# Moving the quarter sums of weights to VectorE inside the scan's slots, and one PSUM bank swapped

## The chip, the cores and the metric

The kernel runs on one core of a Trainium2 chip. The metric is the device time of one execution in microseconds. TensorE (PE in the profile, its weight loads PEld) multiplies matrices, VectorE (DVE) and GpSimd (POOL) do elementwise work, ScalarE (ACT) does activations and scaled copies, and SyncE (SP) issues the DMAs, in one queue, in order.

## The reference

One layer of a network: a layer norm of x (2048 tokens by 1024 channels, float32), then the sum of x, a state-space block and a feed-forward block with routed low-rank adapters, both fed with the normed x.

```python
xn = layernorm(x)
# state-space block: 64 heads of 64, state 128, 8 groups of B and C
proj = xn @ in_proj_w.T                 # gate 4096 | x, B, C 6144 | dt 64
xBC  = silu(causal_conv4(proj[xBC]) + conv_bias)
dt   = softplus(proj[dt] + dt_bias);  dA = exp(-dt * exp(A_log))
state = state * dA_t + (dt_t * x_t) B_t ;  y_t = state C_t    # over tokens t
y = y + x * D
y = groupnorm_rms(y) * norm_weight * silu(gate)
attn = y @ out_proj_w.T
# feed-forward: base product, and the two best of 8 adapters of rank 16
w = softmax over the top 2 of xn @ W_router.T
ffn = xn @ W_base.T + b_base + sum_e w_e * (xn A_e.T) B_e.T * 2
out = x + attn + ffn
```

## The kernel before

**Sections, blocks, slots.** The 2048 tokens lie in two sections of 1024. A section has, for each of the 8 groups, two halves of 512 tokens; section, group and half make a block, 32 in all. A block has four chunks of 128 tokens, c = 0 to 3. One chunk is a slot of the main loop, 128 slots in all. A slot takes some 14 to 18 us.

**Products with seven instead of eight parts.** The large products are made by a scheme of the Strassen kind: a pair of weight tiles is taken as a 2 x 2 matrix of quarters a11, a12, a21, a22, and seven products (PSUM tiles ps_a, ps_x, ps_y) of sums of quarters replace eight. The sums of the weights are s1 = a21 + a22, s2 = s1 - a11, s3 = a11 - a21 and s4 = a12 - s2. A quarter is 128 x 512 float32, 256 KB. In the first section such sums are made on GpSimd as the weights come (L465) and are kept in DRAM.

**What a slot does.** TensorE gets three to five of the seven-part products of the projection (`products`, L81), and among them the scan of the chunk. `scan_a` prepares the next chunk: the scan of the decays es on VectorE (L749, from dab, loaded by DMA and broadcast), ps_cb on TensorE (B times C, and a transpose of B), copies cbm and bt out of it on ScalarE (L760, L762), D times x into ps_y on ScalarE (L767), the masking product of es and cbm on VectorE (L772, kept in the list `masked`), then transposes ps_xt, and xdt and xdd on ScalarE (L784, L792). `scan_b` finishes the chunk: ps_y, then ps_e (C times the state), then ps_st on TensorE; on VectorE ecp times ps_e (L831), the sum with ps_y into xg (L832), and the state (L846), whose decay is a product on GpSimd (L85 with state,tot). In the slots of c = 1 to 3 the convolution of the next block runs: a scaled copy on ScalarE (L698), three steps on VectorE for each of six tiles (L704), a silu on ScalarE (L692). In the slots of c = 3 and 0 the finished block is squared and normed (L872, L875, L876, ps_nv on TensorE, L884 with a table load on ScalarE, L890, L893, L903) and stored.

**Order.** TensorE's instructions keep the order of the program. On VectorE those that are passed to `pin` keep their order among themselves; the scheduler puts the others between them. `behind(a, b)` makes an instruction come after another in the order, with no wait on a semaphore. On GpSimd `gp(1, ...)` keeps the order of the program.

**The quarter sums in question.** Twelve slots, 53 to 64 (the four of each of the last three blocks of the first section), also make sums of weights for later: four pairs of W_base (`base_sums`, tiles wb) and eight pairs of gate weights (`oct_sums`, tiles ws). The generator `quad_sums` has three steps: four loads into one of two "quad" tiles, four sums in place, four stores (L919, L85, L928). The four loads are issued at the end of the slot before, the sums follow `scan_b` in the program's order of the slot, and the stores come at its end, ahead of the next four loads. Four more pairs of gate weights (o = 2) are summed much later, outside the slots. The sums of the output projection's weights, `out_sums`, run from slot 65 on, four on GpSimd and four on VectorE behind the masking product.

**The step sizes' product.** In the last slot of a block, four times in the first section (slots 8, 20, 32 and 44), a piece of the next section's tokens is multiplied with the 200 columns of weights for dt, the router and the adapters: ps_sm, 5.4 us of products, then a copy on ScalarE (L1191). Its PSUM bank has the tag "aux", which ps_cb, ps_nv and the sums of the layer norm use too. The bank with the tag "e" holds ps_e.

## Time and profile before

| | |
|---|---|
| time, median of 3 runs | 3407.71 us (3406.72 to 3408.86) |
| the profiled execution's own time | 3409.37 us |
| its span in the profile | 3407.6 us, at a mean granted clock of 0.996 |
| PE busy | 3351.6 us (98%) |
| DVE busy | 2474.4 us (73%) |
| ACT busy | 1522.1 us (45%) |
| POOL busy | 779.9 us (23%) |
| GB/s, mean | 235 |

How to read it: a share is an average over stages. The slots end near 2100 us of the span; the 48 sums that the change moves run on GpSimd from 999.8 to about 1194 us, and ps_sm stands at 297.0, 484.4, 674.1 and 865.1 us. "A <- B" in a line of waits says that A was idle until B ended. The profile's line numbers are those of the kernel before. L81 and L85 are lines of helpers (every product, every GpSimd sum through `gp`), so tiles tell more there than lines.

### The profile page before, as it was taken

How to read it: one execution, taken by the hardware profiler on the slowest of the kernel's cores; microseconds unless marked ns; L12 is line 12 of the kernel's file. 1: busy time of each engine (PE TensorE's matmuls, PEld its weight loads, DVE VectorE, ACT ScalarE, POOL GpSimd, SP SyncE). 2: the span in 40 equal slices, each digit the busy share in tenths (PEclk: the TensorE clock that was granted, in tenths of full speed). 3: DMA queues.
4: the chain of work that ended last, by engine and by line, in shares of the span. 5: the costliest groups of instructions: out<-in, count | busy, mean ns of one | idle time of the engine just before them, and what ended most of it. 6: DMA issues, size and time to landing. Idle time of an engine off the chain costs nothing.

```text
span 3407.6 us, 41304 instructions
## 1 busy us (share of the span) xinstructions
PE 3351.6 (98%) x13828; PEld 2181.4 (64%) x13828; DVE 2474.4 (73%) x2640; ACT 1522.1 (45%) x4030; POOL 779.9 (23%) x547
## 2 busy tenths in 40 slices
PE   9999999999999999999999999999999999999999
PEld 7455554555554445555555554688888888888888
DVE  7379888889888788898898897555644565556554
ACT  2256766676666566666666664222222200000000
POOL 4122222222214421121212121475444100000000
PEclk9999999999999999999999999999999999999999
DMA  6656666666689988989898899666655787585654
GB/s 247 198 162 220 196 201 194 205 202 200 200 281 312 311 271 272 273 247 290 245 280 254 267 288 303 208 223 232 225 184 185 257 305 242 200 300 179 216 165 144
DMA packets 535571, 799.38 MB, mean 235 GB/s; under 512 B 34880, under 2 KB 264384, under 8 KB 531776
## 3 DMA queue, kind: packets, MB, share of 16 engines
q1 hardware_dynamic: 535360, 796.75, 72.7%
q8 instruction: 111, 1.82, 0.2%
q14 instruction: 100, 0.82, 0.1%
HBM read 546.00 MB, written 250.61 MB: 234 GB/s over the span
## 4 chain that ended last, share of the span: by engine, by line
PE 77%; DVE 12%; ACT 4%; DMA 3%; issue 3%; SPq 0%; POOL 0%; DVEq 0%; ACTq 0%; POOLq 0%
PE ps_x_x L81 11%; PE ps_x_w L81 9%; PE ps_a_x L81 7%; PE ps_y_x L81 7%; PE ps_a_w L81 6%; PE ps_y_w L81 6%; PE ps_x_z L81 5%; DVE xg L704 3%; PE ps_y_z L81 3%; PE ps_a_z L81 3%; PE ps_e L81 3%; PE ps_y L81 3%; PE ps_st L81 2%; PE ps_x_b L81 2%; DVE es L749 2%
## 5 line engine op out<-in xcount | busy, mean ns | idle before, releaser
L85 POOL TENSOR_TENSOR state<-state,tot 128x512 f32<-128x512 f32 x112 | 137.3, 1226 | 951.8 <-PE ps_e L81 898.3
L704 DVE SCALAR_TENSOR_TENSOR xg<-rawx,cw,xg 128x512 f32<-128x512 f32 x384 | 342.2, 899 | 16.8 <-ACT xg L698 5.9
L749 DVE TENSOR_TENSOR_SCAN es<-dab,here 128x1024 f32<-128x1024 f32 x128 | 297.8, 2326 | 14.5 <-DMA dab<-da_d 10.2
L81 PE MATMUL ps_x_w<-t,w 128*128 128x256 f32 x1344 | 303.8, 379 | 0.0
L767 ACT ACTIVATE ps_y<-xg,dsk 128x128 f32<-128x128 f32 x512 | 189.7, 370 | 225.2 <-DVE xg L832 190.0
L81 PEld LDWEIGHTS ps_x_w<-t,w 128*128 128x128 f32 x1344 | 255.4, 190 | 41.5 <-issue 7.4
L792 ACT ACTIVATE xdd<-xdt,es 128x64 f32<-128x64 f32 x1024 | 262.6, 392 | 1.3 <-DVE es L749 1.3
L784 ACT ACTIVATE xdt<-ps_xt,dt 128x64 f32<-128x64 f32 x1024 | 223.8, 337 | 59.1 <-PE ps_xt L105 58.9
L81 PE MATMUL ps_a_w<-q,w 128*128 128x256 f32 x896 | 204.3, 381 | 3.4 <-DMA w<-w 3.4
L704 DVE SCALAR_TENSOR_TENSOR bc<-rawb,cw,bc 128x512 f32<-128x512 f32 x192 | 191.0, 1001 | 18.4 <-ACT bc L698 15.0
L1680 ACT COPY ps_x_w<-ps_a_w 128x512 f32<-128x512 f32 x28 | 16.0, 570 | 420.8 <-PE ps_a_w L81 420.8
L81 PEld LDWEIGHTS ps_a_w<-q,w 128*128 128x128 f32 x896 | 171.3, 191 | 27.4 <-issue 3.8
L81 PEld LDWEIGHTS ps_y<-dab,xdt 128*64 128x64 f32 x2048 | 111.3, 136 | 104.0 <-ACT xdd L792 88.9
L81 PE MATMUL ps_a_x<-op_again,a_x 128*128 128x512 f32 x384 | 176.1, 602 | 0.0
L81 PE MATMUL ps_y_x<-op_again,s_x 128*128 128x512 f32 x384 | 174.4, 597 | 0.0
L81 PE MATMUL ps_x_x<-op_again,s_x 128*128 128x512 f32 x384 | 172.7, 592 | 0.0
L772 DVE TENSOR_TENSOR dab<-es,cbm 128x1024 f32<-128x1024 f32 x128 | 164.8, 1287 | 10.3 <-ACT cbm L760 10.0
L81 PE MATMUL ps_a_x<-op,a_x 128*128 128x512 f32 x368 | 165.5, 592 | 0.0
L81 PE MATMUL ps_y_x<-op,s_x 128*128 128x512 f32 x368 | 165.5, 592 | 0.0
L81 PE MATMUL ps_x_x<-op,s_x 128*128 128x512 f32 x368 | 165.5, 592 | 0.0
L465 POOL TENSOR_TENSOR s_x<-a_x,a_x 128x512 f32<-128x512 f32 x48 | 74.3, 1548 | 363.6 <-PE ps_y_x L81 218.5
L831 DVE TENSOR_TENSOR ecp<-ecp,ps_e 128x512 f32<-128x512 f32 x120 | 81.8, 682 | 103.9 <-PE ps_e L81 97.8
(322 smaller groups left out, 6769.5 us busy)
## 6 DMA issues: line engine op xcount, KB each, us to landing
w<-w SPq DMA_DIRECT2D x196, 512.0 KB, 3.7
dab<-da_d SPq DMA_DIRECT2D x128, 512.0 KB, 6.5
raw<-ev SPq DMA_DIRECT2D x192, 256.0 KB, 4.3
a_x<-in_w_in_dram SPq DMA_DIRECT2D x168, 256.0 KB, 4.9
w<-wo SPq DMA_DIRECT2D x96, 448.0 KB, 4.9
ecp<-run_d SPq DMA_DIRECT2D x256, 128.0 KB, 6.0
y<-xg SPq DMA_DIRECT2D x64, 512.0 KB, 4.5
rawx<-raw SPq DMA_DIRECT2D x24, 1030.0 KB, 7.0
```

The lines of the kernel that those rows point to most:

```text
L81: tc.keep_in_program_order(nc.tensor.matmul(*args, **kw))
L85: ins = nc.gpsimd.tensor_tensor(*args)
L465: nc.gpsimd.tensor_tensor(t[what], t[x], t[y], alu)
L704: ins = nc.vector.scalar_tensor_tensor(dst[:, i, :], raw[:, i, k : k + TB], cw[:, ti, k : k + 1], dst[:, i, :], ALU.mult, ALU.add,)
L749: ins = nc.vector.tensor_tensor_scan(es.rearrange("p h t -> p (h t)"), dab.rearrange("p h t -> p (h t)"), here, 0.0, ALU.mult, ALU.add,)
L767: nc.scalar.activation(psy[:, j, :], xg[:, j, cs], AF.Copy, scale=dsk[:, at : at + 1])
L772: nc.vector.tensor_tensor(ms, es, cbm.unsqueeze(1).to_broadcast([P, HG, Q]), ALU.mult)
L784: ins = nc.scalar.activation(xdt[:, h, :], x_t[:, h, :], AF.Copy, scale=dt_of[s][:, half * NQ + c, at : at + 1],)
L792: ins = nc.scalar.activation(xdd[:, h, :], xdt[:, h, :], AF.Copy, scale=es[:, h, Q - 1 : Q])
L831: pin(nc.vector.tensor_tensor(ecp, ecp, pse, ALU.mult))
L1680: nc.scalar.copy(px, pa)
```

## The change

Three things are edited.

- `quad_sums` takes the function that makes a sum. `base_sums`, and `oct_sums` for o = 0 and 1, pass `add_in_slot`: a sum on VectorE, ordered behind the slot's masking product and pinned. The four pairs of o = 2 stay on GpSimd. `out_sums` uses the new helper for its four VectorE sums; what it makes is the same, but the first of them alone had been ordered behind the masking product, and now all four are.
- The step of the sums in a slot moves from behind `scan_b` to the list `parts[2]`, that is, into the product after the masking product.
- ps_sm moves from the bank "aux" to the bank "e".

In the built program TensorE's order is the same. On VectorE the 48 sums stand, in each slot, behind L772 and what is pinned of the convolution or the norm around it, ahead of L831; in the slot at 1053 us of the old trace the four sums and the copy L829 now stand ahead of the next scan L749, and in the slot at 1110 us the quarter sum L569 of ps_x_x stands ahead of L832, the state and the scan. On GpSimd only the state products are left in the twelve slots. In SyncE's queue one store of the first pair goes ahead of two stores of y.

```diff
+    def add_in_slot(*args):
+
+        ins = nc.vector.tensor_tensor(*args)
+        behind(ins, masked[0])
+        pin(ins)
+
-    def quad_sums(t, quarters, to):
+    def quad_sums(t, quarters, to, add):
...
-        yield from quad_sums(t, halves(w_base[2 * i], w_base[2 * i + 1]), to)
+        yield from quad_sums(t, halves(w_base[2 * i], w_base[2 * i + 1]), to, add_in_slot)
...
-    def oct_sums(pool, o, i):
+    def oct_sums(pool, o, i, add=add):
...
-        yield from quad_sums(t, halves(w_in[at], w_in[at + 2]), to)
+        yield from quad_sums(t, halves(w_in[at], w_in[at + 2]), to, add)
...
-        ins = nc.vector.tensor_tensor(x, t0, t2, ALU.subtract)
-        behind(ins, masked[0])
-        pin(ins)
-        pin(nc.vector.tensor_tensor(t2, t2, t3, ALU.add))
-        pin(nc.vector.tensor_tensor(t0, t2, t0, ALU.subtract))
-        pin(nc.vector.tensor_tensor(t1, t1, t0, ALU.subtract))
+        add_in_slot(x, t0, t2, ALU.subtract)
+        add_in_slot(t2, t2, t3, ALU.add)
+        add_in_slot(t0, t2, t0, ALU.subtract)
+        add_in_slot(t1, t1, t0, ALU.subtract)
...
-                quads += [oct_sums(wq, o, k) for o in range(2) for k in range(4)]
+                quads += [oct_sums(wq, o, k, add_in_slot) for o in range(2) for k in range(4)]
...
             scan_b(*blk, c)
             if c == 0 and prev:
                 norm_mean(*prev)
-            if 0 < q <= len(quads):
-                next(quads[q - 1])
...
                 if b >= 16:
                     parts[2] += [lambda: next(left_sums)]
+            if 0 < q <= len(quads):
+                parts[2] += steps(quads[q - 1], 1)
             products(1, parts[1])
             next(a, None)
             products(1, parts[2])
...
-                ps = ps_one.tile([P, 2, NSM], F32, tag="aux", name=f"ps_sm_{piece[1]}")
+                ps = ps_one.tile([P, 2, NSM], F32, tag="e", name=f"ps_sm_{piece[1]}")
```

## The prediction

> **What bounds the kernel now.** I read the page first, then the stages, the waits of TensorE, and single stretches of the timeline. Two lines of the page, busy time and the chain that ended last:

> ```profile
> PE 3351.6 (98%) x13828; PEld 2181.4 (64%) x13828; DVE 2474.4 (73%) x2640; ACT 1522.1 (45%) x4030; POOL 779.9 (23%) x547
> PE 77%; DVE 12%; ACT 4%; DMA 3%; issue 3%; SPq 0%; POOL 0%; DVEq 0%; ACTq 0%; POOLq 0%
> ```

> TensorE bounds the kernel as a whole, and its order of instructions is the same in both programs. So the change can only win what TensorE loses near the two edits: idle time, and time at half clock. The answer by stages shows both. The columns are the length, the busy time (and count) of PE, PEld, DVE, ACT and POOL, then the granted clock, the DMA share and GB/s. The four short rows are stretches at half clock; the long one holds all 48 sums that the change moves:

> ```profile
> 674.10:677.50 3.40, 3.38 (x10) 3.39 (x11) 2.63 (x3) 3.40 (x15) 0.00 (x0) 0.50 0.96 305
> 1063.20:1066.60 3.40, 3.40 (x5) 1.35 (x5) 3.40 (x2) 1.22 (x5) 0.00 (x0) 0.50 1.05 399
> 1114.40:1121.20 6.80, 5.84 (x7) 2.52 (x8) 5.42 (x6) 0.84 (x4) 0.93 (x1) 0.50 1.02 354
> 1182.70:1186.10 3.40, 3.40 (x5) 1.35 (x4) 2.01 (x2) 3.37 (x12) 0.00 (x0) 0.50 1.06 342
> 985.00:1200.00 215.00, 204.53 (x773) 102.94 (x772) 171.07 (x159) 129.15 (x371) 87.93 (x60) 0.97 0.93 303
> ```

> The waits of TensorE in that long stretch (total us, times, longest):

> ```profile
> PE ps_x_x L81 <- DVE ev L569: 3.7, 1, 3.7
> PE ps_cb L81 <- ACT rms L884: 3.3, 1, 3.3
> PE ps_xt L105 <- DVE state L846: 1.4, 3, 1.1
> PE ps_xt L105 <- ACT xg L692: 1.3, 1, 1.3
> PE ps_y L81 <- ACT xdd L792: 0.7, 1, 0.7
> ```

> They sum to 10.4 us. The half clock costs half of 3.4 + 6.8 + 3.4 us, another 6.8. So TensorE loses 17.2 us among the 48 sums, and VectorE, or ScalarE behind VectorE, ends nearly all of it. Why VectorE is late there shows in the timelines of VectorE and GpSimd (start, length, what, count):

> ```profile
> 1082.42 3.77 DVE L704 SCALAR_TENSOR_TENSOR bc<-rawb,cw,bc 128x512 f32<-128x512 f32 x5
> ...
> 1089.62 4.98 DVE L704 SCALAR_TENSOR_TENSOR xg<-rawx,cw,xg 128x512 f32<-128x512 f32 x3 [3.43 <-DMA raw<-ev]
> ```

> ```profile
> 1089.43 6.31 POOL L85 TENSOR_TENSOR ws<-ws 128x512 f32<-128x512 f32 x4
> ```

> The same convolution step takes 0.75 us while GpSimd rests and 1.66 us while GpSimd sums weights. VectorE's operations that read PSUM (L831, L832, L846) stay at 0.68 us beside GpSimd. Two more rows carry the prices, of the weight sums on GpSimd and of a VectorE sum of this very shape:

> ```profile
> L85 POOL TENSOR_TENSOR wb<-wb x16: 1260/1539/3126, 999.8 to 1057.5; 128x512 f32<-128x512 f32 x16
> ```

> ```profile
> L876 DVE TENSOR_TENSOR sq<-sq x32: 666/683/685, 237.2 to 2119.9; 128x512 f32<-128x512 f32 x32
> ```

> The second edit is about two waits on TensorE's timeline:

> ```profile
> 671.90 0.44 PE L105 MATMUL ps_xt<-ident,xg 128*128 128x128 f32 x2 [0.98 <-ACT xg L692]
> 674.12 2.37 PE L81 MATMUL ps_sm<-wsm,piece 128*128 128x200 f32 x6 [1.77 <-ACT bt L762]
> ...
> 865.10 1.11 PE L81 MATMUL ps_sm<-wsm,piece 128*128 128x200 f32 x5 [1.53 <-ACT bt L762]
> ```

> **Part one: the bank of the step sizes.** ps_sm runs four times, at 297.0, 484.4, 674.1 and 865.1 us. In bank "aux" it waits until ScalarE has copied cbm and bt out of ps_cb. TensorE has no gap before the first two, 1.77 and 1.53 us before the others. In bank "e" its predecessor is ps_e, which VectorE reads at L831. That was done at 859.8 for the last one, and by 668.8 for the third, 5 us early: no wait is left. The price could come at the other end, since the next ps_e now waits for ScalarE's copy of ps_sm (L1191, 0.49 us). That copy began within 0.4 us of the last product's end, and ps_e comes one product of 3.44 us and ps_y of 1.02 us later: covered by over 3 us. Idle 3.30 us; the half clock after the third (its 0.98 us wait stays, and single gaps of 1.1 us elsewhere, at 480.4, drew none) is half of 3.4, 1.7. Sum 5.0 us. [...]

> **Part two: the 48 sums.** Twelve slots, four sums each, leave GpSimd, which keeps only the state's products (L85, 1.04 us alone). VectorE gains 48 x 0.683 = 32.8 us. It loses the slowing: L704 took 16.93, 19.54 and 18.87 us for 18 each in 985-1060, 1060-1130 and 1130-1200, against 27.46 us for 36 in 880-985, so 55.3 - 41.2 = 14.1 us; the gated norm's L893 took 4.83, 3.74 and 4.75 us for four against 2.72 without GpSimd at 1202.7, so 5.2 us; L903 3.20 and 4.50 against 2.35 for two, so 3.0 us. Net +10.5 us: 171.1 to 181.6 us of a stretch that would shrink from 215 to about 198 us, 92%. That is close, but 1200-1320 us has 107.7 of 120 (90%) and loses one gap of 2.0 us. The price of a sum is bounded by 0.68 (GpSimd at rest) and 1.37 us (doubled, as L704 is); I take 0.68, since only one state product a slot is left there.

> No row shows the new sums' own wait. They stand in VectorE's queue behind the masked product (L772), after the conv steps or norm around them, and wait for four loads issued at the end of the slot before; behind a waiting sum stand the conv steps, ecp, xg, the state and the next scan, and behind those ScalarE's ps_y and TensorE's transposes. When the loads had landed shows where GpSimd waited for them, against the end of the VectorE work that now stands ahead: 999.8 against 1006, 1022.5 against 1021.7, 1038.7 against 1038.7, 1053.5 against 1052.0, 1068.6 against 1072, 1102.9 against about 1104, 1132.7 against 1139, 1189.2 against 1188.5. So it waits 0 to 1.5 us, and the 1.5 lies inside a wait of 4.54 us for dab. In the slots of 1086 and 1155 the sums fill waits of 3.43 and 4.07 us that VectorE has before the xg steps.

> What each place of loss becomes:
> - 1062.59, 3.26 us and 1.7 at half clock. The chain was: dab lands late, the scan runs at 1056.58, and only behind it the copy xg L829 at 1059.47, ps_y, a table load, rms at 1061.85, ps_cb. In the new order the copy stands before that scan, behind the four sums: sums from 1053.5 to 1056.2, copy to 1056.9, ps_y, table load and rms (0.37 + 1.28 + 0.69) to 1059.3, just when TensorE gets there (1059.3). Won: 5.0.
> - 1096.6 to 1115.4, 0.17 + 0.72 + 3.73 and 3.4 at half clock. VectorE's xg steps ran 4.98 us for three and 8.89 for seven. Unslowed they are 2.2 and 5.2; the first slot's sums lie in the 3.43 us wait, the second's add 2.7. So ev arrives about 2.8 + 3.7 - 2.7 = 3.8 us earlier by this alone, and the new order sets it ahead of the scan and the squares. Won 7.3, with the 0.72 for ScalarE's xdd left in place.
> - 1165.1 to 1182.2, 0.17 + 1.06 + 1.31 and 1.7 at half clock. Steps of 4.54 for three and 9.45 for eight become 2.2 and 5.9, with one slot's sums uncovered: 2.3 + 3.5 - 2.7 = 3.1 us against 2.5 us of waits. That is thin: I count half, 2.1.

> SyncE's queue moves with it. The stores L928 waited 26.5 us in all for GpSimd's ws sums, with the next loads, dab, ecp and raw behind them. At 1090.7 to 1096.1 they will go some 6 us earlier; where a norm is in the slot, one store goes ahead of the two of y, and the rest follow as before. The bytes are the same. VectorE's four waits for the state product behind the sums (6.9 us up to 1215) go too. [...] The state products mostly run while VectorE does ecp and xg, which read PSUM; the longest took 3.39 us.

> Sum: 5.0 + 5.0 + 7.3 + 2.1 = 19.4; I take off 2.0 for small new waits (the 0.5 to 0.8 us landings above): 17.4 us. The profiled execution took 3409.37 us, 3407.6 of span and 1.8 around it; it becomes 3392.0. It lies 1.7 us over the median of 3407.71, which becomes 3390.3 us.

> **Rivals.**
> 1. VectorE becomes the bound of the conv slots. Scan 2.2, masked product 1.1, nine steps 6.7, two ev 1.2, ecp, xg and state 1.9 are 13.1 us; the sums make 15.8, where TensorE's slot with three products is about 14.1. For it: six such slots. Against it: in the old trace ecp ran 6.2 us behind ps_e at 1094.5 before a transpose waited 0.17 us, so two slots in a row stay inside the slack. If so, the bank and 1062.59 win 10, the rest nothing: 3398.
> 2. The sums change nothing: their waits come back elsewhere, and the bank's 5.0 is all: 3402.7.
> 3. Slower: the loads land late. Median landing of ws is 5.0 us, the longest 10.7; at 94% DMA share more can be late. From about 1 us later than in the old trace, VectorE stands still at the slots of 1022, 1038 and 1189, where no other wait covers it, and TensorE follows past the slack of 6 us. At 10.7 us each is 4.5 us late: 13.5, and the bank's gain: 3416.
> 4. The half clock stays, drawn by the small waits that are left, such as the 0.98 us one at 671.9: 8.5 us less, 3398.8, counted in with rival 1. Or the bank's wait is only passed on to ps_e: 3395, inside the forecast's spread.

> **How the numbers follow.** A measurement here can tell about 0.2%, 6.8 us, from no change. Forecast, gains of 12 to 23 us: 0.56. Rival 1: 0.17. Rival 2: 0.15. Rival 3: 0.12. Faster is 0.56 + 0.17 = 0.73, same 0.15, slower 0.12. The low end is all 22.2 us and the 2.0 us gap at 1229.2 with some of its half clock: 3383. The high end takes in rival 2 with two thirds of its spread: 3407. It leaves out rival 3 and some 0.06 of the others.

> **What would show it.** Right: L704 back near 0.75 us between 985 and 1200; GpSimd's L85 rows wb gone, VectorE's there at 0.68; no TensorE gap over 1 us at the four places, no half clock there; ps_sm without a wait; VectorE near 182 us in the stretch. Wrong: VectorE waiting for wb or ws loads by more than 2 us with TensorE waiting behind it; ps_e waiting for L1191; the gap at 1115 still there behind ev.

## The result, and the profile after

The changed kernel takes 3399.77 us (median of 8 runs, 3392.98 to 3403.31), and the kernel before, run beside it, 3408.28 us (3406.72 to 3413.09). The ratio is 0.997, with a 95% interval of 0.9959 to 0.9981. The kernel is faster, by 8.5 us where 17.4 were forecast. The profiled execution took 3401.96 us, 3400.1 of it span.

The two lines of the page, busy time and the chain that ended last, stand nearly as before; VectorE has 15 us more, GpSimd 77 us less:

```profile
PE 3344.5 (98%) x13828; PEld 2178.1 (64%) x13828; DVE 2489.8 (73%) x2688; ACT 1523.0 (45%) x4030; POOL 703.3 (21%) x499
PE 72%; DVE 14%; DMA 6%; ACT 5%; issue 3%; SPq 0%; POOL 0%; DVEq 0%; ACTq 0%; POOLq 0%
```

TensorE executes the same instructions in the same order in both programs, so each of its instructions can be set against itself in the other trace: its start after minus its start before is the **shift**. The work between 985 and 1200 us of the old trace lies between 990.78 and 1190.34 of the new one. The answer by stages for that stretch (length, busy time and count of PE, PEld, DVE, ACT, POOL, then granted clock, DMA share, GB/s), and below it the waits of TensorE there:

```profile
990.78:1190.34 199.56, 197.94 (x774) 101.24 (x773) 184.58 (x208) 129.74 (x374) 14.70 (x12) 1.00 1.00 332
```

```profile
PE ps_xt L105 <- DVE state L846: 1.1, 1, 1.1
PE ps_y L81 <- ACT xdt L784: 0.4, 1, 0.4
```

215 us have become 199.6, its three half-clock stretches of 3.4 to 6.8 us are gone (the clock is 1.00), and 10.4 us of waits have become 1.5. VectorE is busy 184.6 us of it, 92%. The groups of the convolution step and of the sums (minimum, median and maximum in ns; L918 is the line of `add_in_slot` in the changed kernel):

```profile
L704 DVE SCALAR_TENSOR_TENSOR xg<-rawx,cw,xg x37: 724/752/1414, 984.4 to 1170.2; 128x512 f32<-128x512 f32 x37
L918 DVE TENSOR_TENSOR wb<-wb x16: 679/691/928, 1012.1 to 1059.9; 128x512 f32<-128x512 f32 x16
L918 DVE TENSOR_TENSOR ws<-ws x32: 678/692/1521, 1073.1 to 1182.1; 128x512 f32<-128x512 f32 x32
```

So in this stretch nearly everything went as forecast; of the waits named beforehand one is left, the 1.06 us before a transpose (at 1180.5 us before, at 1173.0 now). The shift tells where the rest of the gain went. It is +2.9 us at 660 us, where nothing has been edited yet: that is the difference of two executions. Behind the third ps_sm it falls to -1.0, and at 709 us it is +3.1 again. Behind the fourth it falls from 3.8 to 2.0, and is 5.8 at 936 us. Through the sums it falls from +5.8 to -10.2 and by 1234 to -12.2, since the half clock behind the wait at 1229 is gone (the wait itself only shrank, from 2.0 to 1.7 us); it is -9.7 at 1290 and -7.8 at the end. **The sums won about as much as forecast; the bank's gain was won twice and lost twice, each time within 70 us.** At the fourth ps_sm twice as much was lost as won, 3.8 us against 1.8. TensorE's timeline at these places:

```profile
674.91 5.58 PE L81 MATMUL ps_sm<-wsm,piece 128*128 128x200 f32 x32
...
692.42 0.49 PE L81 MATMUL ps_cb<-bc 128*128 128x128 f32 x2 [2.12 <-ACT rms L884]
...
902.90 3.70 PE L81 MATMUL ps_x_x<-op,s_x 128*128 128x512 f32 x8 [0.89 <-ACT s_x L520]
...
937.22 0.63 PE L105 MATMUL ps_xt<-ident,xg 128*128 128x128 f32 x4 [2.52 <-DVE state L846]
```

ps_sm waits no more, and 18 us behind it TensorE waits 2.12 us for the norm's rms, then runs 3.4 us at half clock (693.3 to 696.7). VectorE's and ScalarE's timelines show what rms waited for:

```profile
680.98 2.29 DVE L749 TENSOR_TENSOR_SCAN es<-dab,here 128x1024 f32<-128x1024 f32 x1 [1.96 <-ACT xdd L792]
683.19 0.27 DVE L337 TENSOR_TENSOR scr<-sm,dtb 128x128 f32<-128x128 f32 x1
...
688.43 0.15 DVE L427 TENSOR_TENSOR m_b<-m_b,m_a 128x2 f32<-128x2 f32 x1
688.50 0.68 DVE L829 COPY xg<-ps_y 128x512 f32<-128x512 f32 x1
```

```profile
689.22 0.37 ACT L767 ACTIVATE ps_y<-xg,dsk 128x128 f32<-128x128 f32 x1 [2.12 <-DVE xg L829]
...
690.39 1.28 ACT L884 ACT_TABLE_LOAD   x1
691.68 0.69 ACT L884 ACTIVATE rms<-ps_nv,eps 128x512 f32<-128x512 f32 x1
```

The copy L829 could run at 685.0, when the products into ps_y end. Twenty-three small operations on ps_sm's result (step sizes L337 to L347, the choice of experts L408 to L427) stand ahead of it for 5.3 us. The start of this chain hangs on ScalarE's xdd, not on ps_sm. An earlier ps_sm brings TensorE sooner to the place where it needs rms, and nothing else moves.

At 937 the chain is longer. VectorE is busy without a break from 873.5 to 905 us, with the small operations of the fourth ps_sm among its work, so its convolution steps start no earlier than with the old bank: 35.2 us behind the transposes ps_xt ahead of ps_sm, against 35.1 in the kernel with the sums alone (Experiments). GpSimd, released by TensorE's ps_e and ps_y_x, comes 0.6 us earlier (counted in the same way), and its work now falls beside three of the 18 steps in place of one (1.41, 1.69 and 1.83 us; the others take 0.75). The steps take 16.1 us in place of 14.4 and end late, at 926.86. SyncE's timeline has the next load of rawx waiting for that, and a load of a_g behind it:

```profile
926.89 0.37 SPq L679 DMA_DIRECT2D rawx<-raw  x1
927.31 0.50 SPq L461 DMA_DIRECT2D a_g<-in_w_in_dram  x1
```

GpSimd's weight sum waits for this a_g; behind the sum stands the state's product, and behind that VectorE's state:

```profile
934.09 1.26 POOL L465 TENSOR_TENSOR s_g<-a_g,s_g 128x512 f32<-128x512 f32 x1 [8.15 <-DMA a_g<-in_w_in_dram]
```

### The profile page after: what moved, and what is told of

It is laid out like the page before. It is cut to its first block, busy times and chain, and to the rows that moved or that the text cites. A ratio compares the mean times of both kernels' runs of the same rounds, so it can differ in the third digit from the quotient of the medians.

```text
span 3400.1 us, 41266 instructions
## 1 busy us (share of the span) xinstructions
PE 3344.5 (98%) x13828; PEld 2178.1 (64%) x13828; DVE 2489.8 (73%) x2688; ACT 1523.0 (45%) x4030; POOL 703.3 (21%) x499
## 4 chain that ended last, share of the span: by engine, by line
PE 72%; DVE 14%; DMA 6%; ACT 5%; issue 3%; SPq 0%; POOL 0%; DVEq 0%; ACTq 0%; POOLq 0%
PE ps_x_x L81 10%; PE ps_x_w L81 8%; PE ps_y_x L81 6%; PE ps_a_x L81 6%; PE ps_y_w L81 5%; PE ps_a_w L81 5%; PE ps_x_z L81 5%; PE ps_y_z L81 3%; PE ps_a_z L81 3%; DVE xg L704 3%; PE ps_e L81 2%; PE ps_y L81 2%; PE ps_st L81 2%; PE ps_x_b L81 2%; DVE es L749 2%
## 5 line engine op out<-in xcount | busy, mean ns | idle before, releaser
L85 POOL TENSOR_TENSOR state<-state,tot 128x512 f32<-128x512 f32 x112 | 136.5, 1219 | 1085.0 <-PE ps_e L81 1003.3
L704 DVE SCALAR_TENSOR_TENSOR xg<-rawx,cw,xg 128x512 f32<-128x512 f32 x384 | 331.2, 870 | 9.6 <-ACT xg L698 2.3
L749 DVE TENSOR_TENSOR_SCAN es<-dab,here 128x1024 f32<-128x1024 f32 x128 | 296.1, 2313 | 10.8 <-ACT xdt L784 5.7
L81 PE MATMUL ps_x_w<-t,w 128*128 128x256 f32 x1344 | 303.8, 379 | 0.0
L81 PEld LDWEIGHTS ps_x_w<-t,w 128*128 128x128 f32 x1344 | 255.4, 190 | 41.5 <-issue 7.4
L792 ACT ACTIVATE xdd<-xdt,es 128x64 f32<-128x64 f32 x1024 | 262.6, 392 | 1.4 <-DVE es L749 1.4
L81 PE MATMUL ps_a_w<-q,w 128*128 128x256 f32 x896 | 202.7, 379 | 5.1 <-DMA w<-w 5.1
L704 DVE SCALAR_TENSOR_TENSOR bc<-rawb,cw,bc 128x512 f32<-128x512 f32 x192 | 186.5, 977 | 20.8 <-ACT bc L698 17.3
L81 PEld LDWEIGHTS ps_a_w<-q,w 128*128 128x128 f32 x896 | 170.1, 190 | 28.8 <-issue 5.8
L81 PEld LDWEIGHTS ps_y<-dab,xdt 128*64 128x64 f32 x2048 | 112.4, 136 | 105.7 <-ACT xdd L792 83.9
L772 DVE TENSOR_TENSOR dab<-es,cbm 128x1024 f32<-128x1024 f32 x128 | 165.5, 1293 | 13.2 <-ACT cbm L760 12.8
L81 PE MATMUL ps_x_x<-op_again,s_x 128*128 128x512 f32 x384 | 172.7, 592 | 0.0
L81 PE MATMUL ps_a_x<-op_again,a_x 128*128 128x512 f32 x384 | 172.7, 592 | 0.0
L81 PE MATMUL ps_y_x<-op_again,s_x 128*128 128x512 f32 x384 | 172.7, 592 | 0.0
L81 PE MATMUL ps_x_x<-op,s_x 128*128 128x512 f32 x368 | 167.3, 598 | 0.9 <-ACT s_x L520 0.9
L81 PE MATMUL ps_y_x<-op,s_x 128*128 128x512 f32 x368 | 165.5, 592 | 0.0
L81 PE MATMUL ps_a_x<-op,a_x 128*128 128x512 f32 x368 | 165.5, 592 | 0.0
L81 PE MATMUL ps_y<-dab,xdt 128*64 128x128 f32 x2048 | 143.3, 279 | 7.6 <-ACT xdd L792 3.9
L831 DVE TENSOR_TENSOR ecp<-ecp,ps_e 128x512 f32<-128x512 f32 x120 | 81.8, 682 | 93.0 <-PE ps_e L81 88.2
```

What stands on the lines that cost most here:

```text
L81: tc.keep_in_program_order(nc.tensor.matmul(*args, **kw))
L85: ins = nc.gpsimd.tensor_tensor(*args)
L704: ins = nc.vector.scalar_tensor_tensor(dst[:, i, :], raw[:, i, k : k + TB], cw[:, ti, k : k + 1], dst[:, i, :], ALU.mult, ALU.add,)
L749: ins = nc.vector.tensor_tensor_scan(es.rearrange("p h t -> p (h t)"), dab.rearrange("p h t -> p (h t)"), here, 0.0, ALU.mult, ALU.add,)
L772: nc.vector.tensor_tensor(ms, es, cbm.unsqueeze(1).to_broadcast([P, HG, Q]), ALU.mult)
L792: ins = nc.scalar.activation(xdd[:, h, :], xdt[:, h, :], AF.Copy, scale=es[:, h, Q - 1 : Q])
```

## Experiments

Theory A: the gain is that of the sums, and it comes from the engine and from the order. Theory B: ps_sm's wait of 3.1 us was slack, since the chain of small operations behind it ends no earlier; it hands the gain on. Rival C: the bank costs by itself, since ps_e and ps_sm now wait for one another. Every kernel ran beside the kernel before. Each expectation names the theories as they stood when it was written: the "Rival B" of the first three is a rival of their theory A, and not theory B of this list.

**Each part alone.** The sums with the old bank, then the bank with the old sums:

```
sums only (the changed kernel, but):
    ps = ps_one.tile([P, 2, NSM], F32, tag="aux", name=f"ps_sm_{piece[1]}")
bank only (the kernel before, but):
    ps = ps_one.tile([P, 2, NSM], F32, tag="e", name=f"ps_sm_{piece[1]}")
```

> The change with ps_sm left in bank aux: the 48 sums on VectorE alone. Theory A (the sums win, the bank's win comes back): in the change's profile TensorE's lead grows from +5.8 us behind to 9.7 us ahead between 985 and 1267 us, 15.5 us, and the bank ends at about 0; so this kernel is at 3393 to 3396, as fast as the change or faster by up to 2 us, and its shift against before from 985 to 1267 us is again -14 to -17 us. Rival B (both halves win, and the sums win only half of what was forecast): the shift over that stretch is near -5 us in most executions and the kernel is about 3.5 us slower than the change, 3403.

> The kernel before with ps_sm in bank e: the bank alone. Theory A: ps_sm starts 1.8 and 1.5 us earlier at 674 and 865 us, but behind the third one ps_cb then waits for rms L884 (2.1 us in the change's profile, and half clock after it), since the copy L829 stands behind the small operations of the step sizes on VectorE; net 0 to -2 us, 3406 to 3408.5. Rival B: the full 5.0 us of the forecast, 3403.

Sums alone: 3394.06 us (ratio 0.9957, 0.9944 to 0.9969), 14.4 us faster than before. Bank alone: 3411.22 us (1.0005, 0.9997 to 1.0014), no gain at all; a gain of 5.0 us would be 0.9985. TensorE's waits between 660 and 960 us, with the sums alone and with the bank alone:

```profile
PE ps_sm L81 <- ACT bt L762: 3.1, 2, 1.7
...
PE ps_cb L81 <- ACT rms L884: 0.6, 1, 0.6
```

```profile
PE ps_cb L81 <- ACT rms L884: 3.0, 2, 2.2
PE ps_xt L105 <- DVE state L846: 2.6, 1, 2.6
...
PE ps_x_x L81 <- ACT s_x L520: 0.9, 1, 0.9
```

With bank "aux" 3.1 us in front of ps_sm and 0.6 behind; with "e" nothing in front and 6.5 behind (5.5 in the changed kernel). The bank by itself moves the loss and enlarges it. And the half clock behind the third ps_sm, which my price of the bank held, is not there with the sums alone, though ps_sm waits 1.34 us there.

**Room and place of the sums.** One kernel, made from the kernel before, leaves the 48 sums out (the quarters are stored unsummed), the other takes the changed kernel's sums back to their old place in the slot:

```diff
-    def quad_sums(t, quarters, to):
+    def quad_sums(t, quarters, to, add=lambda *a: None):
...
-        yield from quad_sums(t, halves(w_in[at], w_in[at + 2]), to)
+        yield from quad_sums(t, halves(w_in[at], w_in[at + 2]), to, *([add] if o == 2 else []))
```

```diff
+            if 0 < q <= len(quads):
+                next(quads[q - 1])
...
-            if 0 < q <= len(quads):
-                parts[2] += steps(quads[q - 1], 1)
```

> The kernel before without the 48 sums (loads and stores are kept, so what is stored are unsummed quarters): neither GpSimd's slowing nor VectorE's extra work. Theory A: the stretch 985 to 1267 us gains about what the change gains there, 15 to 18 us: 3390 to 3393, so VectorE has room for 33 us more work. Rival B (VectorE is the bound in the conv slots with the sums on it): this kernel gains at least 6 us more over that stretch than the sums on VectorE do.

> The change with the step of the sums at its old place in the program: on VectorE the four sums then stand right behind the state L846 and ahead of the next scan L749, soon after their loads were issued. Theory A: the place matters, because VectorE now waits there for the loads, which land about 5 to 6 us after the issue; some 2 to 4 us of standstill in each of the twelve slots, of which the slack hides part: the gain of the sums is lost, 3405 to 3425. Rival (GpSimd's slowing was all, and any place on VectorE will do): as the change, 3393 to 3400.

Without the sums: 3394.79 us (0.9956, 0.9943 to 0.997), the same as with them on VectorE (3394.06), though above the 3390 to 3393 that I expected. VectorE had the room: its 48 sums cost nothing that these runs can tell. In the old place: 3428.79 us (1.0054, 1.0041 to 1.0066), 29 us above the changed kernel and above the range that I gave. TensorE's waits from 985 to 1225 us there, and one of them on VectorE's and ScalarE's timelines:

```profile
PE ps_y L81 <- ACT xdd L792: 24.0, 7, 7.9
PE ps_y L81 <- ACT bc L698: 4.9, 2, 3.7
```

```profile
1164.00 2.87 DVE L918 TENSOR_TENSOR ws<-ws 128x512 f32<-128x512 f32 x4 [4.04 <-DMA ws<-in_w_in_dram]
1166.79 2.29 DVE L749 TENSOR_TENSOR_SCAN es<-dab,here 128x1024 f32<-128x1024 f32 x1
```

```profile
1169.17 2.03 ACT L792 ACTIVATE xdd<-xdt,es 128x64 f32<-128x64 f32 x8 [5.50 <-DVE es L749]
```

Written ahead of the scan, the sums wait 4.04 us for their loads; behind them stands the scan, behind it xdd, and behind it TensorE. This is the mechanism of my slower rival, and it is the place behind the masked product that keeps it away: there VectorE waits 1.7 and 1.2 us for loads, and TensorE waits for neither.

**Engine or order.** The kernel before with the sums left on GpSimd, only their step moved to where the change has it; and the kernel before with nothing but the copy L829 put into VectorE's written order, ahead of the next scan:

```diff
-            if 0 < q <= len(quads):
-                next(quads[q - 1])
...
+            if 0 < q <= len(quads):
+                parts[2] += steps(quads[q - 1], 1)
```

```diff
-            nc.vector.tensor_copy(xg[:, :, cs], psy)
+            pin(nc.vector.tensor_copy(xg[:, :, cs], psy))
```

> The kernel before with the sums left on GpSimd and only their step moved to the third part of the slot, where the change has it. If the engine is what counts (VectorE's steps slowed beside GpSimd), L704 stays at 1.4 to 1.8 us beside the sums, the waits behind ev and xg near 1096 to 1115 and 1165 to 1182 stay, and the time is 3402 to 3412 us. If the place alone is what counts, 3393 to 3397 us as with the sums on VectorE.

> The kernel before with the copy L829 (first chunk of a group) put into the written order of VectorE, so that it stands ahead of the next scan at all eight groups. My step says that of the sums' gain 5.0 us (a wait of 3.26 us and half of 3.4 us at half clock near 1062 us) come from this order: 3402 to 3405 us, without a wait before ps_cb near 1062. If the order of the copy is not the cause, the wait stays, 3406 to 3409 us. Scans that now stand behind a late copy could cost elsewhere: up to 3412 us.

On GpSimd in the new place: 3408.51 us (0.9997, 0.9988 to 1.0006). The engine counts: L704's median over the stretch is 1.30 us, and the wait for ev keeps its length:

```profile
L704 DVE SCALAR_TENSOR_TENSOR xg<-rawx,cw,xg x36: 725/1296/1749, 1021.2 to 1175.4; 128x512 f32<-128x512 f32 x36
```

```profile
PE ps_x_x L81 <- DVE ev L569: 3.7, 1, 3.7
PE ps_cb L81 <- ACT rms L884: 2.2, 1, 2.2
```

With the copy in the written order: 3407.6 us (0.9993, 0.9985 to 1.0002), not the 3402 to 3405 that I expected, and below what a measurement can tell. In its trace the wait near 1062 us and the half clock behind it are gone, and the shift against the kernel before falls from +0.8 to -4.3 there: 5.1 us for the 5.0 of my step. It keeps them up to 2060 us and gives 3.0 back by 2080, at a wait for xdd that lasts 3.88 us there and 2.52 in the kernel before, and with half clock behind it (1.7 us) that the kernel before does not have there. VectorE's timeline at the place:

```profile
1054.83 0.69 DVE L829 COPY xg<-ps_y 128x512 f32<-128x512 f32 x1 [2.27 <-PE ps_y L81]
1056.06 2.84 DVE L749 TENSOR_TENSOR_SCAN es<-dab,here 128x1024 f32<-128x1024 f32 x1 [0.54 <-DMA dab<-da_d]
```

The copy no longer stands behind a scan whose dab is late.

**The chain behind ps_sm: a first try.** If theory B holds, the bank's gain stays once the small operations are out of the way. Here three of them, and so all behind them, are held behind the work that is written ahead of them, with bank "e" and with bank "aux":

```diff
+        def held(ins):
+            return pinned and behind(ins, pinned[-1])
...
-        nc.vector.tensor_scalar(u2, u, 2.0, None, ALU.add)
+        held(nc.vector.tensor_scalar(u2, u, 2.0, None, ALU.add))
```

and the same at L408 and L424.

> The changed kernel (bank e, sums on VectorE), with VectorE's small operations on the step sizes and the experts' choice (L344, L408, L424 and what hangs on them) held behind the work that is written ahead of them, where the scheduler had drawn them forward. The order on TensorE is the same. Theory B (the earlier ps_sm wins 3.1 us, and the chain sm, small operations, copy L829, ps_y, rms, ps_cb on VectorE and ScalarE gives them back): the waits of 2.1 us for rms before ps_cb near 690 us, 0.9 us for s_x near 900 us and 2.5 us for the state near 935 us go, no wait before ps_sm comes back, time 3389 to 3393 us. Rival C (the bank e itself costs, since ps_e and ps_sm now wait for one another): the three waits stay and the time stays at 3398 to 3402 us. If the held operations crowd the slots of the convolution, both this kernel and the next have new waits there.

> As the kernel before it in this list, but with ps_sm in bank aux: the control for what the held order does by itself. Theory B: the waits before the third and fourth ps_sm are there again (1.3 and 1.7 us), nothing comes after them, 3392 to 3396 us, about 3 us above its twin with bank e (without the held order bank e was 5.7 us worse). Rival C: this kernel is 4 to 6 us better than its twin, as without the held order.

3432.31 us (1.0069, 1.0056 to 1.0082) and 3437.82 us (1.0081, 1.0067 to 1.0095): the edit itself costs over 30 us against the changed kernel, where I had expected 3389 to 3393 and 3392 to 3396. The waits at 690, 900 and 935 are gone with bank "e", but the step sizes now come so late that ScalarE's exponential L357 waits for them with the scan's xdt queued behind it:

```profile
931.10 0.31 ACT L357 ACTIVATE ex<-at 128x128 f32<-128x128 f32 x1 [7.15 <-DVE at L356]
931.32 1.73 ACT L784 ACTIVATE xdt<-ps_xt,dt 128x64 f32<-128x64 f32 x8
```

The sign between the banks is turned round, as theory B has it, but the intervals overlap, and with such new waits around this decides nothing.

**The chain behind ps_sm: the narrow edit.** Only the second part of the step sizes and the choice of experts are held, and only behind the last copy L829; then the same with bank "e" for the first three ps_sm and "aux" for the fourth, and with "aux" for all:

```diff
+        def held(ins):
+            return s and behind(ins, copied[0])
...
-            nc.vector.tensor_copy(xg[:, :, cs], psy)
+            copied[:] = [nc.vector.tensor_copy(xg[:, :, cs], psy)]
```

with `held` around L344 and L408 alone.

> The changed kernel with a narrower edit than the held order: the second part of the small operations (from L344) and the experts' choice (from L408) stand behind the last copy L829, and nothing else is held. Near 690 us the copy then stands third behind sm's first operations; behind the fourth ps_sm the thirteen operations of the choice (some 2.5 us of VectorE) and L424 to L433 move out of the busy stretch 873 to 905 into the group after it. Theory B: no wait of 2.1 us for rms before ps_cb near 690 us and none for s_x near 900 us, the one for the state near 935 us under 1 us; the bank's 3.1 us stay won: 3388 to 3392 us. Rival C (bank e itself costs): 3398 to 3402 us with the waits still there. Each choice needs one more table load of 1.28 us on ScalarE, which could cost up to 1.3 us a time, 5 us in all: 3393 to 3397 us.

> As the kernel before it in this list, with ps_sm in bank e the first three times and in bank aux the fourth: orders on all engines are the same. Theory B: 1 to 2 us slower than it, since the fourth ps_sm waits 1.5 us again and nothing behind it comes late any more: 3389 to 3394 us. Rival C: the fourth's part of the loss goes, about 2.4 us faster than it.

> As the first kernel of this list, with ps_sm in bank aux all four times. Theory B: about 3 us slower than it, with waits of 1.3 and 1.7 us before the third and fourth ps_sm and nothing behind them: 3391 to 3395 us. Rival C: 4 to 6 us faster than it, as without the edit.

The times are 3390.24 us (0.9944, 0.9932 to 0.9957) with bank "e", 3388.60 (0.994, 0.9926 to 0.9953) mixed, and 3390.07 (0.9948, 0.9935 to 0.996) with "aux". Against the changed kernel (0.9959 to 0.9981) the intervals of bank "e" lie apart: the same bank, the same sums, and about 9.5 us less by moving small operations behind a copy. So the bank itself is no cost, and rival C falls, which the traces below bear out. VectorE's and TensorE's timelines and TensorE's waits from 660 to 960 us, bank "e":

```profile
679.23 0.23 DVE L342 TENSOR_SCALAR scr<-scr 128x128 f32<-128x128 f32 x1
679.49 0.69 DVE L829 COPY xg<-ps_y 128x512 f32<-128x512 f32 x1
```

```profile
684.60 0.38 PE L81 MATMUL ps_cb<-bc 128*128 128x128 f32 x2
```

```profile
PE ps_st L81 <- ACT xdd L792: 1.3, 2, 0.9
PE ps_cb L81 <- ACT mean L278: 0.7, 1, 0.7
```

The copy runs as soon as ps_y is there, ps_cb does not wait, and the waits for s_x and the state are gone. What the bank is then worth the traces show and the times don't. In the profile with "aux" the waits in front of ps_sm are back:

```profile
PE ps_sm L81 <- ACT bt L762: 2.8, 2, 1.5
```

Its shift against the one with "e" grows by 1.6 and 1.8 us at the third and fourth ps_sm and is not given back by 1260 us; but the medians of the three kernels, and that of the sums alone (3394.06), differ by less than these intervals can tell. Theory B's order of the three times was missed: the mixed kernel is 1.6 us faster than the one with "e", not 1 to 2 slower, and "aux" is 0.2 us faster, not about 3 slower.

The traces of four kernels together decide between B and C at both places. Counted from the start of the transposes ps_xt ahead of ps_sm, TensorE comes to its next late meeting after (us, one execution each):

| | sums alone ("aux") | changed kernel ("e") | narrow edit, "aux" | narrow edit, "e" |
|---|---|---|---|---|
| third ps_sm, to ps_cb behind rms | 18.0 | 17.9 | 17.2 | 15.7 |
| fourth ps_sm, to ps_xt behind the state | 68.6 | 70.4 | 68.1 | 66.3 |

Without the narrow edit bank "e" wins nothing at the third and loses 1.8 us at the fourth; with it, it wins 1.6 and 1.8. The kernel without the sums (18.0 and 68.6) agrees with the first column, and the one with the bank alone (18.1 and 71.3) with the second. With bank "e" and the narrow edit the convolution steps at the fourth start 32.7 us behind ps_xt, only one of the 18 is slowed, and they take 14.4 us again. Whether the mixed kernel, the fastest median of all, is really the best stays open.

## Why the prediction was right in sign and wrong in size

- **What bounds the kernel:** right. All of the gain lies in TensorE's waits and half clock at the edits.
- **The price of the sums:** right. I had 14.4 us for them (5.0 + 7.3 + 2.1), before the 2.0 taken off; alone they won 14.4 in time. That the two agree to the tenth is luck: the interval of the time is 10.6 to 19.1 us, and in the trace of that kernel the shift falls by 17.5 us from 985 to 1200 and gives some 3 back later. By the shift, place by place in the changed kernel: near 1062 from +5.9 to +0.6, so 5.2 for 5.0; from 1096 to 1122, 7.9 for 7.3; from 1165 to 1200, 2.9 for 2.1. The new waits of 0.4 and 1.25 us at 1177 and 1251 are the sort that the 2.0 stood for.
- **The operations:** 48 sums took 36.8 us (11.2 + 25.6) for 32.8 forecast; L704 41.8 us (28.6 + 13.2) for 54 steps, for 41.2. VectorE has 184.6 us in 199.6, for 181.6 in 198.
- **The bank's 5.0 us:** wrong, and it is the step that failed. Alone it won nothing, which rules 5.0 us out. With the sums it made the time worse, by 5.7 us in the medians (3394.06 to 3399.77, with intervals that overlap) and by 3.7 us in the traces between 660 and 985 us. It had two faults. The 3.3 us of waits were taken as a loss that ends when the bank is free; I looked for the next late thing at the bank (ps_e behind L1191, "passed on to ps_e") and not on TensorE's next wait for VectorE, the one for rms behind sm, the small operations and L829. That chain was already due: with the sums alone it ends 0.6 us late, though ps_sm's waits are still there. And the 1.7 us of half clock were read from one execution: there one window of 3.4 us held 2.75 us of waits (0.98 and 1.77), while the sums-alone kernel, with its wait of 1.34 us at this place, has no half clock.
- **The size of the whole:** the measured time lies 9.5 us above the forecast's 3390.3, and inside its range only because the high end, 3407, had taken in part of rival 2; the forecast itself meant gains of 12 to 23 us.
- **Rival 1**, VectorE as the bound, gave 3398 and the result is near it; still it falls, since leaving the sums out wins nothing more. **Rival 2**, only the bank wins, was the opposite of what happened. **Rival 3**, late loads, did not come here, and the sums in their old place show that its mechanism is real and dear. **Rival 4**, the half clock stays, gave 3398.8, and that it is near is luck: of the 8.5 us of half clock that were counted, the 6.8 among the sums went, and the 1.7 behind the third ps_sm came back 19 us later, at 693.3. Its second half, the bank's wait passed on, was right in kind, but not to ps_e.
- **The half clock.** The terms among the sums were rightly counted: before the change 3.4 us at half clock stood behind waits of 3.26 us at 1062.6 and of 1.06 and 1.31 us near 1181, and after it 3.4 us follow a wait of 2.12 us at 692.4. What counts in the traces is how much of a window of 3.41 us is idle (last section).
- **The sums beside GpSimd's state products.** The twelve state products on GpSimd in the stretch took 14.7 us, 2.2 more than at 1.04 each. The sums took 4.0 us more than at rest, the longest 1.52 us. No wait of TensorE's in the stretch stands behind a lengthened sum: its two are at 1173.0 and 1177.5, and the sums of that slot, from 1165.9, took 2.86 us for four.

## What to carry to other kernels

Before a wait is counted as won, follow TensorE forward to its next meetings with the other engines and ask how far each is from being late, and whether what it waits for starts any earlier; where it doesn't, the wait was slack and comes back there. Work of a third engine that follows the earlier one can also come to stand beside other steps and slow them, as GpSimd's did here. Price small elementwise operations by what stands behind them in the queue, not by their own length: 5 us of them ahead of one 0.7 us copy cost more than 48 sums of 0.7 us that stood behind everything urgent. And when two edits come together, measure each alone first: here one was worth 14 us and the other took some 4 to 6 of them back.

## What the runs showed of the hardware

```profile
689.88:693.29 3.41, 1.29 (x6) 0.63 (x6) 3.21 (x12) 3.35 (x7) 0.00 (x0) 1.00 0.91 349
693.29:696.70 3.41, 3.41 (x6) 1.34 (x5) 3.41 (x2) 0.58 (x3) 0.00 (x0) 0.50 0.23 82
```

```profile
685.10:688.51 3.41, 1.86 (x5) 0.56 (x3) 3.31 (x16) 2.49 (x5) 0.00 (x0) 1.00 1.10 389
688.51:691.92 3.41, 2.72 (x9) 1.52 (x10) 3.31 (x5) 2.11 (x6) 0.00 (x0) 1.00 0.40 153
```

- The same program's executions lie up to 12 us apart (3403.66 to 3415.33 for the bank alone), with shifts of 2 to 3 us in stretches that no edit touches; inside one trace the shift at an edit is far sharper than the time.
